# A sum's limit on another engine, quotients behind a small reciprocal, and weights scaled by another engine, in a two-layer convolution kernel

## The chip, the cores and the metric

The kernel runs on one core of one Trainium2 chip. The metric is the device time of one execution in microseconds (us); the time of a version is the median of its runs. The core has TensorE (PE, matrix products), VectorE (DVE), ScalarE (ACT), GpSimd (POOL) and queues for transfers. Each engine works through its own instructions in the order in which they stand in its program, and waits at an instruction until what it needs is there.

## The reference, cut to what matters

The input is 8 images of 256 channels of 64x64 pixels. Two layers are added to it in turn, each on a group-normalised input. Layer 0 makes 9 weights per pixel and channel group from small convolutions and applies them to a 3x3 neighbourhood. Layer 1 has an attention over a 7x7 neighbourhood and a dynamic convolution, whose part is what the change touches:

```python
# layer 0: 1x1 convolutions of the normalised input
x1 = _conv1x1(x, w1, b1)
x2 = _conv1x1(x, w2, b2)
x3 = _conv1x1(x, w3, b3)
...
# layer 1
wts = jnp.einsum('oc,bchw->bohw', Wfc, x).reshape(b, C, kc2, h, w)
wts = jax.nn.softmax(wts, axis=2)
...
oc = _dwconv(hid, w2).reshape(b, kc2, C, h, w)
out_conv = jnp.sum(oc * wts.transpose(0, 2, 1, 3, 4), axis=1)
return rate1 * out_att + rate2 * out_conv
```

The nine copies of `oc` that the softmax weighs are equal, so the kernel makes one. It takes the exponentials of eight differences to the ninth logit, adds them and 1 into `tot`, limits that, and weighs `oc` with `tot` times its reciprocal `rec`. In layer 0 the normalisation is folded into the weights: `w12` and `w3` are multiplied per input channel by `sc`, once for each image.

## The kernel before, in words

An image is cut into 8 bands of 8 rows (512 pixels). Channels lie on the 128 partitions in two tiles, `ct` 0 and 1. The main loop goes over bands `g` and in each over 8 steps `s`; `ct = s // 4` and `m = s % 4`. I call the four steps of one `ct` a half. In one iteration, layer 1 of band `g` is worked on, and layer 0 of a band twelve ahead, so that both layers share the engines.

The order of the work is written out by hand. A step has six places, one for each call of `advance()`; a function handed to `after(n, f)` is put into the programs n places later. So a number in `after` is a position in every engine's queue and not a time.

In each step:

- TensorE applies the attention weights of two steps before (`sco`, L747), makes this step's scores (`sco`, L703), transposes the probabilities of the step before (`ptp`, L735), and makes two products with the weights of the dynamic convolution (`pf`, L825, each shown as four matmuls of 128x512); then come layer 0's products (`p` L369, `pw` L447, `ph` L429) and the maps of queries, keys and values (`pq` L637, `pk` L658, `pv` L563).
- VectorE takes the scores' maximum (`prob`, `nmax`, L712), adds attention values to the output (`xr`, L757), does taps of two depthwise convolutions (`acc`, L782 and L808), and inverts the sum of the attention's exponentials. This is the small reciprocal: `tot`, L727, two columns. It also makes the products of layer 0 (`prod`, L460).
- ScalarE copies the transposed probabilities (`pt`, L737), makes the attention's exponentials (`prob`, L720), the exponentials of `pf` (`ex`, L830, twice a step), and multiplies the probabilities by the small reciprocal (`prob`, L729). In its order these stand as L737, L720, first L830, L729.
- GpSimd adds layer 0's products up (`xg`, L468) and the exponentials of a half's steps (`ex`, L1026).

At the end of a half (m = 3) `dynamic_sum` follows, which the change touches. Its parts before, by the step counted from the half's last one, which is step 0:

- step 1, place 2: GpSimd adds the two columns of `ex` (L838) into `tot`, which is `ex[:, 1]`.
- step 2, place 1: `quotient`: VectorE adds 1 and limits the sum (L845), and inverts the first half of it (L846). At place 4 `second` inverts the other half (L850). I call this step A.
- place 0 that ends step 2: `weigh`: GpSimd multiplies (L855, L856) and adds to the output (L857). The step that follows is B, and the one after it C.

The tile `ex` has three buffers and each step takes one: the `ex` of step B is written by L830 into the buffer that L855 and L856 of the half have read. `rec` has one buffer, `prod` two, and the PSUM tiles tagged `gen` five.

For `ct` 0 step A is `s` 5 of the same band, for `ct` 1 it is `s` 1 of the next band. Step `s` 0 of a band also starts the small maps of layer 0 (`p`, L328), whose eight evictions (L343, L347) ScalarE does in step 0 and 1.

`scaled_weights` is called once an image; its `scale` multiplies `w12` and `w3` (L296, L297), two tiles each.

Of the kernel before, what the change touches and what calls it, by code (L numbers as in the profile page):

```python
# [12 lines left out]
AF = mybir.ActivationFunctionType  # L13
ALU = mybir.AluOpType
# [72 lines left out]
def conv_layers_kernel(ctx: ExitStack, tc: tile.TileContext, ins: dict, out: bass.AP):  # L87
    nc = tc.nc
# [18 lines left out]
    def load(name, shape, src=None, now=True):  # L107
        t = const.tile(shape, F32, name=f"c_{name}")
        late.append(lambda: nc.scalar.dma_start(out=t, in_=ins[name] if src is None else src))
        if now:  # L110
            late.pop()()
        return t
# [5 lines left out]
    w12 = load("w12", [P, NCT, 2 * REL], ins["w12"].rearrange("(t p) n -> p t n", p=P))  # L118
    w3 = load("w3", [P, NCT, C], ins["w3"].rearrange("(t p) n -> p t n", p=P))
# [95 lines left out]
    def after(n, f):  # L215
        later.append((place[0] + n, f))
# [8 lines left out]
    def gn_affine(sts, means, name, done):  # L225


        n = len(sts)
        mv = stat.tile([P, n, 2], F32, name=f"mv_{name}", tag=f"mv{n}")
        for ct, st in enumerate(sts):  # L230
            nc.vector.bn_aggr(mv[:, ct, :], st)
        mean, var = mv[:, :, 0], mv[:, :, 1]
        gm, d, sc, bi = (stat.tile([P, n], F32, name=f"{v}_{name}", tag=f"{v}{n}") for v in ("gm", "d", "sc", "bi"))

        def group_means(v, k):
            pg = ps.tile([P, n], F32, name=f"pg_{name}_{k}", tag="gen", bufs=5)
            nc.tensor.matmul(pg, means, v, start=True, stop=True)
            return pg


        def a1():
            pg = group_means(mean, 0)
            after(2, lambda: a2(pg))

        def a2(pg):
            nc.vector.tensor_copy(gm, pg)
            for ct in range(n):
                c = slice(ct, ct + 1)
                nc.vector.tensor_scalar(d[:, c], pg[:, c], mean[:, c], None, ALU.subtract)
                nc.vector.tensor_scalar(d[:, c], d[:, c], d[:, c], var[:, c], ALU.mult, ALU.add)  # L250
            after(5, a3)

        def a3():
            pg = group_means(d, 1)
            after(2, lambda: a4(pg))

        def a4(pg):
            nc.vector.tensor_scalar(sc, pg, GN_EPS, None, ALU.add)
            after(2, a5)

        def a5():
            nc.scalar.activation(sc, sc, AF.Sqrt)
            after(4, a6)

        def a6():
            nc.vector.reciprocal(sc, sc)
            for ct in range(n):
                c = slice(ct, ct + 1)
                nc.vector.tensor_scalar(bi[:, c], gm[:, c], sc[:, c], -1.0, ALU.mult, ALU.mult)
            done(sc, bi)  # L270

        after(3, a1)
# [15 lines left out]
    def scaled_weights(b):  # L288

        im = images[b]  # L290

        def scale(sc, bi):
            im.w12s = w0.tile([P, NCT, 2 * REL], F32, tag="w12s", name=f"w12s_{b}", bufs=1)
            im.w3s = w0.tile([P, NCT, C], F32, tag="w3s", name=f"w3s_{b}", bufs=1)
            for kt in range(NCT):
                nc.vector.tensor_scalar(im.w12s[:, kt], w12[:, kt], sc[:, kt : kt + 1], None, ALU.mult)  # L296
                nc.vector.tensor_scalar(im.w3s[:, kt], w3[:, kt], sc[:, kt : kt + 1], None, ALU.mult)  # L297
            after(5, lambda: through(bi))

        def through(bi):  # L300
            pb = ps.tile([P, 1 + NCT], F32, tag="gen", name=f"pb_{b}", bufs=5)
            for m, to, w in ((0, 0, w12), (0, 64, w12), (1, 0, w3[:, :, :P]), (2, 0, w3[:, :, P:])):
                for kt in range(NCT):
                    nc.tensor.matmul(
                        pb[to : to + w.shape[2], m : m + 1], w[:, kt], bi[:, kt : kt + 1],
                        start=(kt == 0), stop=(kt == NCT - 1),
                    )
            after(2, lambda: biases(pb))

        def biases(pb):  # L310
            im.bias = w0.tile([P, 1 + NCT], F32, tag="bias", name=f"bias_{b}")
            nc.vector.tensor_add(im.bias[:, 0:1], pb[:, 0:1], par[:, PB21 : PB21 + 1])
            for ct in range(NCT):
                nc.vector.tensor_add(
                    im.bias[:, 1 + ct : 2 + ct], pb[:, 1 + ct : 2 + ct], chan[:, ct, CB3 : CB3 + 1]
                )

        gn_affine([im.st0[:, ct] for ct in range(NCT)], gmat, f"a{b}", scale)

    def small_maps(b, i):  # L320
# [396 lines left out]
    def exponentials(nm, prob, nmax):  # L717
        tot = w1.tile([P, 2], F32, tag="tot", name=f"tot_{nm}", bufs=4)
        for h in range(2):
            nc.scalar.activation(  # L720
                prob[:, h, :NKEY], prob[:, h, :NKEY], AF.Exp, bias=nmax[:, h : h + 1], scale=-1.0,
                accum_out=tot[:, h : h + 1],
            )
        return tot
# [107 lines left out]
    def dynamic_sum(b, i, ct, ex, oc):  # L832

        tot = ex[:, 1]
        xr = images[b].xr[i]

        engine = nc.vector if (b, i, ct) == (B - 1, NB - 1, NCT - 1) else nc.gpsimd
        engine.tensor_add(tot, tot, ex[:, 0])  # L838
        rec = w1.tile([P, BAND], F32, tag="rec", name=f"rec_{b}_{i}_{ct}", bufs=1)
        n = BAND // 2  # L840

        def quotient():


            nc.vector.tensor_scalar(tot, tot, 1.0, 1.0e37, ALU.add, ALU.min)  # L845
            nc.vector.reciprocal(rec[:, :n], tot[:, :n])  # L846
            after(3, second)

        def second():
            nc.vector.reciprocal(rec[:, n:], tot[:, n:])  # L850
            after(2, weigh)

        def weigh():

            engine.tensor_mul(tot, tot, rec)  # L855
            engine.tensor_mul(oc, oc, tot)  # L856
            engine.tensor_add(xr[:, ct], xr[:, ct], oc)  # L857
            if ct == NCT - 1:
                after(6, store)

        def store():
            nc.sync.dma_start(
                out=out[b].rearrange("(t p) n -> p t n", p=P)[:, :, i * BAND : (i + 1) * BAND], in_=xr
            )

        after(5, quotient)


    def beside(g, s):
# [93 lines left out]
    with tc.manual_schedule():  # L963
# [21 lines left out]
        for g in range(-AHEAD, B * NB):  # L985
            b, i = divmod(g, NB)
            for s in range(STEPS):
# [3 lines left out]
                if g >= 0:  # L991
# [9 lines left out]
                    tot = exponentials(nm, prob, nmax)  # L1001
# [21 lines left out]
                if g >= 0:  # L1023
                    branch_weights(b, i, ct, m, 1, ex)
                    if exb is not None:
                        after(4, lambda ex=ex, exb=exb: nc.gpsimd.tensor_add(ex, ex, exb))  # L1026
                    if m == 1:
                        conv[1]()
                        conv = depthwise_middle(b, i, ct)
                    if m == NT // 2 - 1:  # L1030
                        oc = depthwise_end(b, i, ct, conv[1])
                        after(4, lambda a=(b, i, ct, ex, oc): dynamic_sum(*a))
# [97 lines left out]
```

## Time and profile before

| What | Value |
|---|---|
| Median of 3 runs | 4154.88 us (4153.21 to 4155.15) |
| Span of the profiled run, granted TensorE clock | 4150.9 us, 0.993 |
| Busy in all: PE, DVE, ACT, POOL | 4022.6, 3591.9, 3081.0, 2923.0 us |
| Busy from 1000 to 2000 us: PE, DVE, ACT, POOL | 988.9, 896.7, 773.0, 749.2 us |
| L845, limit of the sum, DVE, 128x512 | 128 times, mean 1070 ns, median 418 ns |
| L846 and L850, reciprocals, DVE, 128x256 | 128 times each, means 1753 and 1746 ns |
| L727, small reciprocal, DVE, 128x2 | 512 instructions, mean 159 ns |
| L296 and L297, scaling, DVE, 128x64 and 128x256 | 16 times each, means 997 and 1060 ns |
| L838, L855, L856, L857, GpSimd, 128x512 | 127 times each, 1272 to 1278 ns |
| L468, GpSimd, 128x1024 | 549 times, mean 2193 ns |

In the table a mean far above the median says that some instructions of a kind take much longer than others of the same form. The busy time of PE has ends that are modelled, so waits of PE are better read from the starts of its instructions. In the lines of the waits view, "A <- B" says that A's engine stood idle before A until B released it; the figures are the total, the count and, last, the longest.

### The profile page before, as it was taken

The page shows a single profiled execution, that of the slowest core. Times are in us where ns is not written, and L with a number is a line of the kernel's source. Part 1 is how long each engine was busy: PE and PEld are TensorE (multiplying, and loading weights), DVE is VectorE, ACT ScalarE, POOL GpSimd, SP SyncE. Part 2 cuts the span into 40 slices and gives each one's busy share as a digit, 9 for nine tenths or more (in the row PEclk, how much of TensorE's full clock was granted, in tenths as well). Part 3 has the DMA queues.
Part 4 walks back from the last instruction along what each step waited for, and adds up shares of the span by engine and source line. Part 5 has one row for each costly group of instructions (what it writes and reads, how often), then busy time and mean ns, then how long its engine had stood idle before and what let it go on. Part 6 is the DMA issues. An engine that isn't in the chain of part 4 may idle for free.

```text
span 4150.9 us, 72735 instructions
## 1 busy us (share of the span) xinstructions
PE 4022.6 (97%) x25292; PEld 2126.8 (51%) x25292; DVE 3591.9 (87%) x7248; ACT 3081.0 (74%) x7726; POOL 2923.0 (70%) x1902
## 2 busy tenths in 40 slices
PE   6789999999999999999999999999999999999998
PEld 3345555555555555555555555555555555455554
DVE  5878998899898898889998898888988889977777
ACT  3467778777787777877778777777778777687776
POOL 4767777677786777777777777777777677744554
PEclk8999999999999999999999999999999999999999
DMA  8854234234244233334234234244233233111100
GB/s 226 194 135 111 73 91 109 72 94 109 62 101 107 76 94 98 81 94 109 72 85 118 72 94 105 66 101 106 71 82 99 65 87 85 33 41 39 39 28 21
DMA packets 381264, 367.89 MB, mean 89 GB/s; under 512 B 55648, under 2 KB 282720, under 8 KB 380640
## 3 DMA queue, kind: packets, MB, share of 16 engines
q1 hardware_dynamic: 377568, 358.68, 34.3%
q8 instruction: 200, 3.28, 0.3%
q10 hardware_dynamic: 3328, 4.55, 0.3%
q14 instruction: 168, 1.38, 0.1%
HBM read 261.42 MB, written 101.71 MB: 87 GB/s over the span
## 4 chain that ended last, share of the span: by engine, by line
PE 71%; DVE 14%; POOL 6%; ACT 5%; DMA 2%; issue 2%; SPq 1%; POOLq 0%; ACTq 0%; DVEq 0%
PE pf L825 33%; PE ptp L735 5%; PE sco L747 5%; PE pk L658 5%; PE sco L703 5%; PE p L369 5%; DVE prod L460 4%; PE pq L637 4%; POOL xg L468 3%; PE pvt L607 2%; PE pv L563 2%; DVE acc L808 2%; PE pw L447 2%; DVE acc L782 2%; POOL ex L1026 2%
## 5 line engine op out<-in xcount | busy, mean ns | idle before, releaser
L825 PE MATMUL pf<-yp,c_wfc 128*128 128x512 f32 x4096 | 1930.5, 595 | 10.6 <-ACT vc L581 5.0
L468 POOL TENSOR_TENSOR xg<-xg,prod 128x1024 f32<-128x1024 f32 x549 | 1203.9, 2193 | 96.6 <-DVE prod L460 64.1
L825 PEld LDWEIGHTS pf<-yp,c_wfc 128*128 128x128 f32 x4096 | 729.9, 190 | 690.5 <-issue 619.4
L1026 POOL TENSOR_TENSOR ex<-ex,ex 128x1024 f32<-128x1024 f32 x384 | 907.7, 2364 | 61.9 <-ACT ex L830 57.2
L830 ACT ACTIVATE ex<-pf 128x512 f32<-128x512 f32 x1024 | 607.3, 593 | 297.9 <-POOL ex L1026 141.3
L782 DVE SCALAR_TENSOR_TENSOR acc<-yp,c_chan,acc 128x504 f32<-128x504 f32 (+3 forms) x1104 | 766.2, 694 | 42.3 <-ACT acc L773 21.7
L460 DVE SCALAR_TENSOR_TENSOR prod<-pw,c_par,x3q 128x1040 f32<-128x1040 f32 x576 | 733.9, 1281 | 66.8 <-PE pw L447 21.6
L808 DVE SCALAR_TENSOR_TENSOR acc<-hid,c_chan,acc 128x504 f32<-128x504 f32 (+3 forms) x1024 | 757.8, 740 | 20.2 <-ACT acc L802 2.1
L855 POOL TENSOR_TENSOR ex<-ex,rec 128x512 f32<-128x512 f32 x127 | 162.3, 1278 | 809.5 <-DVE rec L850 767.1
L729 ACT ACTIVATE prob<-prob,tot 128x196 f32<-128x196 f32 x1024 | 411.6, 450 | 387.2 <-DVE tot L727 386.4
L712 DVE CUSTOM_DVE_ANT_0 prob<-sco,c_mask 128x196 f32<-128x196 f32 x1024 | 325.5, 355 | 272.4 <-PE sco L703 272.0
L720 ACT ACTIVATE prob<-prob,nmax 128x196 f32<-128x196 f32 x1024 | 461.4, 454 | 46.9 <-DVE nmax L712 45.3
L747 PEld LDWEIGHTS sco<-pt,vt 112*64 112x64 f32 x8160 | 283.8, 137 | 182.3 <-issue 51.7
L737 ACT COPY pt<-ptp 112x512 f32<-112x512 f32 x511 | 297.0, 581 | 105.0 <-PE ptp L735 103.0
L735 PE MATMUL ptp<-ident,prob 128*112 128x128 f32 x2044 | 341.7, 287 | 31.2 <-ACT prob L729 30.5
L747 PE MATMUL sco<-pt,vt 112*64 112x64 f32 x8160 | 347.0, 227 | 0.0
L735 PEld LDWEIGHTS ptp<-ident,prob 128*112 128x112 f32 x2044 | 203.9, 133 | 201.4 <-issue 77.7
L703 PE MATMUL sco<-kb,qb 64*64 64x196 f32 x4096 | 295.2, 357 | 0.0
L563 PE MATMUL pv<-yp,c_wv 128*128 128x512 f32 (+2 forms) x576 | 247.3, 554 | 0.6
L369 PE MATMUL p<-xc,w3s 128*128 128x512 f32 x512 | 244.4, 601 | 0.0
L658 PE MATMUL pk<-yp,c_wk 128*128 128x512 f32 (+2 forms) x576 | 240.8, 545 | 0.0
L637 PE MATMUL pq<-yp,c_wq 128*128 128x512 f32 x512 | 240.6, 592 | 0.0
(140 smaller groups left out, 5294.0 us busy)
## 6 DMA issues: line engine op xcount, KB each, us to landing
x<-x3n SPq DMA_DIRECT2D x128, 264.0 KB, 2.1
x3q<-x SPq DMA_DIRECT2D x128, 264.0 KB, 7.2
xc<-in_x SPq DMA_DIRECT2D x64, 512.0 KB, 5.0
xg<-in_x SPq DMA_DIRECT2D x256, 128.0 KB, 4.8
x<-xg SPq DMA_DIRECT2D x256, 128.0 KB, 2.4
yp<-x SPq DMA_DIRECT2D x128, 256.0 KB, 3.3
xr<-x SPq DMA_DIRECT2D x64, 512.0 KB, 5.8
out_x<-xr SPq DMA_DIRECT2D x64, 512.0 KB, 3.1
```

What stands on the lines that cost most here:

```text
L369: nc.tensor.matmul(p3, im.w3s[:, kt, mt * P : (mt + 1) * P], im.xc[i][:, kt, :], start=(kt == 0), stop=(kt == NCT - 1),)
L460: nc.vector.scalar_tensor_tensor(prod[:, :, :RUN], pw[:, j, :RUN].unsqueeze(1).to_broadcast([P, SHARE, RUN]), par[:, PCB2 + k : PCB2 + k + 1],
L468: nc.gpsimd.tensor_add(im.xg[i], im.xg[i], rows(prod))
L703: nc.tensor.matmul(sco[half[t], h, :NKEY], qb[half[h], 2 * m + t].rearrange("p r c -> p (r c)"), kb[half[h], :, c0 : c0 + KW], start=True, ...
L720: nc.scalar.activation(prob[:, h, :NKEY], prob[:, h, :NKEY], AF.Exp, bias=nmax[:, h : h + 1], scale=-1.0, accum_out=tot[:, h : h + 1],)
L735: nc.tensor.transpose(ptp[:, h, ch], prob[:, h, ch * CHUNK : (ch + 1) * CHUNK], ident)
L747: nc.tensor.matmul(po[half[h], :, t * TQ : (t + 1) * TQ], im.vt[i + ch, m][:n, t, (2 * ct + h) * HD : (2 * ct + h + 1) * HD], pt[:n, h, ch ...
L782: nc.vector.scalar_tensor_tensor(o, yp[:, ct, ra + dr : rb + dr, ca + dc : cb + dc], chan[:, ct, CW1 + k : CW1 + k + 1], o, ALU.mult, ALU.add,
L808: nc.vector.scalar_tensor_tensor(o, hid[:, ra + dr : rb + dr, ca + dc : cb + dc], chan[:, ct, CW2 + k : CW2 + k + 1], o, ALU.mult, ALU.add,)
L825: nc.tensor.matmul(pf, wfc[:, kt, 2 * m + j, ct * P : (ct + 1) * P], images[b].yp[i][:, kt, PAD : PAD + R], start=(kt == 0), stop=(kt == N ...
L830: nc.scalar.activation(ex[:, j].rearrange("p (r c) -> p r c", r=R), pf, AF.Exp)
L1026: after(4, lambda ex=ex, exb=exb: nc.gpsimd.tensor_add(ex, ex, exb))
```

## The change

The limit of the sum goes from VectorE to GpSimd and stands right behind the sum it limits (L841 of the changed kernel). The quotient is put in two places later, so that the small reciprocal of that step stands ahead of it on VectorE, and the second half follows it two places later instead of three. The scaling of the 1x1 weights goes from VectorE to ScalarE.

```diff
-                nc.vector.tensor_scalar(im.w12s[:, kt], w12[:, kt], sc[:, kt : kt + 1], None, ALU.mult)
-                nc.vector.tensor_scalar(im.w3s[:, kt], w3[:, kt], sc[:, kt : kt + 1], None, ALU.mult)
+                nc.scalar.activation(im.w12s[:, kt], w12[:, kt], AF.Copy, scale=sc[:, kt : kt + 1])
+                nc.scalar.activation(im.w3s[:, kt], w3[:, kt], AF.Copy, scale=sc[:, kt : kt + 1])
...
         engine.tensor_add(tot, tot, ex[:, 0])
+        engine.tensor_scalar(tot, tot, 1.0, 1.0e37, ALU.add, ALU.min)
...
         def quotient():
-            nc.vector.tensor_scalar(tot, tot, 1.0, 1.0e37, ALU.add, ALU.min)
             nc.vector.reciprocal(rec[:, :n], tot[:, :n])
-            after(3, second)
+            after(2, second)
...
-        after(5, quotient)
+        after(7, quotient)
```

## The prediction, made before the changed kernel was run

> **What bounds the kernel now.** I read the page first: who is busy, and through whom the chain runs.
>
> ```profile
> PE 4022.6 (97%) x25292; PEld 2126.8 (51%) x25292; DVE 3591.9 (87%) x7248; ACT 3081.0 (74%) x7726; POOL 2923.0 (70%) x1902
> ...
> PE 71%; DVE 14%; POOL 6%; ACT 5%; DMA 2%; issue 2%; SPq 1%; POOLq 0%; ACTq 0%; DVEq 0%
> ```
>
> TensorE sets the time, but 29% of the chain is others: somewhere PE waits. Work freed on VectorE is worth only the waits of PE that it ends. I measured these in the PE timeline between 400 and 3900 us, as the start of each group of matmuls less the shortest usual distance from the group before: 88 us in all, about 12.5 us in each image of eight bands (499 us). Of these 64 us lie at the transposes L735 or the pf after them, which need the probabilities of the step before. So I asked who waits in that chain.
>
> ```profile
> POOL ex L855 <- DVE rec L850: 767.1, 119, 15.4
> ...
> ACT prob L729 <- DVE tot L727: 386.4, 266, 6.4
> ...
> ACT ex L830 <- POOL oc L856: 24.5, 58, 1.5
> ```
>
> ScalarE stands before L729 because the small reciprocal L727 comes late; GpSimd stands 767 us idle at L855; and L830, which in ScalarE's order comes ahead of the next L729, already meets GpSimd's L856 with no room left in 58 places. The last line matters most below. Then the timelines. A half of ct 1, first VectorE (start, duration):
>
> ```profile
> 2008.82 0.41 DVE L845 TENSOR_SCALAR ex<-ex 128x512 f32<-128x512 f32 x1
> 2009.27 1.75 DVE L846 RECIPROCAL rec<-ex 128x256 f32<-128x256 f32 x1
> ...
> 2012.30 0.16 DVE L727 RECIPROCAL tot<-tot 128x2 f32<-128x2 f32 x1
> ...
> 2013.87 1.75 DVE L850 RECIPROCAL rec<-ex 128x256 f32<-128x256 f32 x1
> 2015.53 1.20 DVE L460 SCALAR_TENSOR_TENSOR prod<-pw,c_par,x3q 128x1040 f32<-128x1040 f32 x1
> ```
>
> ScalarE in the same half:
>
> ```profile
> 2011.84 0.20 ACT L720 ACTIVATION_READ_ACCUMULATOR prob<-prob,nmax 128x1 f32 x1
> ...
> 2019.08 0.58 ACT L830 ACTIVATE ex<-pf 128x512 f32<-128x512 f32 x1
> 2020.31 0.81 ACT L729 ACTIVATE prob<-prob,tot 128x196 f32<-128x196 f32 x2 [0.65 <-DVE tot L727]
> ```
>
> GpSimd and TensorE there:
>
> ```profile
> 2015.70 1.28 POOL L855 TENSOR_TENSOR ex<-ex,rec 128x512 f32<-128x512 f32 x1 [6.11 <-DVE rec L850]
> 2017.06 1.28 POOL L856 TENSOR_TENSOR oc<-oc,ex 128x512 f32<-128x512 f32 x1
> ```
>
> ```profile
> 2022.66 0.65 PE L735 MATMUL ptp<-ident,prob 128*112 128x128 f32 x4
> ```
>
> L720 ends at 2012.04, so L727 could not have run before that: here the quotient fills a time in which VectorE would have stood. L729 ends at 2021.12 and PE takes its result at 2022.66: 1.5 us to spare.
>
> [...] L845 takes 0.41 us in ct 1 and, in most halves of ct 0, 2.38 us beside an L468 of 2.19 us (mean 1070 ns, median 418). [...]
>
> **The change, part by part.** I set the two programs' instruction orders side by side.
>
> *Scaling.* VectorE loses 15.9 + 17.0 = 32.9 us (L296, L297). [...] It helps VectorE in one half an image.
>
> *The limit.* VectorE loses 136.9 us (L845) and the 33 us wait for L838. GpSimd gains 127 L841. Not in the trace; from below, a copy of 128x420 (L633) takes 536 ns, so 0.65 us for 512 columns; from above a tensor_tensor of 128x512, 1.27. I take 0.8[...]. GpSimd idles there for 5 to 6 us, so its cost is only that L846 of ct 0 may wait for it.
>
> *The quotients.* On VectorE, step A was L845, L846, two taps, L727, two taps, L850, prod, L712; it becomes two taps, L727, L846, two taps, L850, prod, L712. On GpSimd weigh slips one place: in 107 of 127 halves an L468 now stands ahead of L855, and it needs the prod that comes after L850.
>
> ct 1, the half shown: the taps end at 2010.3, L727 waits for L720 until 2012.1, and L846 is queued behind it. L846 12.2 to 13.9, taps to 15.35, L850 to 17.05 (15.62 before). Prod +1.2 = 18.2; L468 +2.2 = 20.4; L855 and L856 +2.63 = 23.1 (18.34 before). L830 of step B waits for that: 23.1 instead of 19.08. Behind it in ScalarE's queue L729 starts 0.5 later, ends 24.4 instead of 21.12. PE can begin its transposes about 0.28 before that end, at 24.1: it stands 1.5 us. The next pf needs the bank that L641, behind L729, frees: 0.4 more, as the ct 0 half at 2053 shows now. The same sum over the rows of the other halves of ct 1 gives 1.3 to 1.8 us in 41 of 54 (the rest have 3.4 us to spare, or no L343 queue): 62 us, with the 0.4 each 78 us. The last ten bands' halves mostly have no L468; there nothing moves the end.
>
> ct 0, the half around 2039: L845 went (2.38 us), L727 comes at 2040.6 instead of 2044.9. PE's waits for that L729 end: 1.5, 0.6 and 1.5 us in each of seven images, 25 us. The later wait, at step C, is 0.41 + 0.44 us in 36 halves. There L838 ended at 2039.44; GpSimd runs 0.6 later against PE after ct 1 (its unbroken run starts 2.55 later, PE stands 1.9), L841 0.8, so L846 at 2040.85 (2041.88 before). Two taps and L727 (1.48) now stand ahead of it, so L850 ends 1.03 + 1.48 = 2.5 earlier, 2045.7. Prod 46.9, L468 49.1, L856 51.75 (50.94): L830 0.8 later, but L729, which waited for L727 until 2052.92, at 52.25. That frees about 0.65 of the 0.85: 36 x 0.65 = 23 us.
>
> Sum: +78 - 25 - 23 = +30 us: 4154.9 + 30 = 4185.
>
> **Rivals.** *Faster.* The GpSimd delay is absorbed and only gains count: -25 - 36 x 0.85 = -56, 4099. For it: VectorE loses 170 us of work and waits, and L729's wait for L727 is 386 us, which the new order attacks directly. Against: L830 stands ahead of L729 in one queue, and its buffer waits for L856. If half the loss comes, 39 - 48 = -9: 4146.
>
> *No change.* Losses and gains cancel within 8 us, 4147 to 4163; nothing couples them, so it is a matter of sizes.
>
> *Worse.* L841 at 1.27 us and GpSimd's lag keep step C's waits of ct 0 and lengthen them by 0.5: 78 - 25 + 18 = +71, 4226. For it: GpSimd has hardly a gap from 2015.70 to 2039.44 in the trace.
>
> *VectorE becomes the bound* by its idle time at L727, 1.7 us in 41 halves: no, it waits for PE's scores 272 us in all, before L712, and catches up there.
>
> **How the numbers follow.** The forecast 0.51; worse 0.20; faster 0.20; no change 0.09. Slower is the first two: 0.71. From the half-absorbed and full gains down to 4125 and up past the worse case to 4235 I leave out some 0.1 below and 0.05 above, and what the hand sums miss in how a wait of PE moves the next.
>
> **What would show it.** Right: in the waits, L830 on L856 rises from 24.5 to over 150 us; L727 on L720 rises from 10.1 to about 70; the wait for L845 is gone; L729 on L727 falls to below half of 386; L855's on L850 falls, taken over by L468 waiting for prod; on GpSimd L468 stands between L841 and L855; PE's idle time at L735 on L729 (107.6 us with its weight loads) rises, in the third step of a band. A step is wrong if L841 takes over 1.3 us, or if L846 of ct 1 doesn't wait behind L727. The forecast is wrong if L830 waits for L856 below 50 us: then ScalarE is not held, and the time falls under 4147.

## The result, and the profile after

| Version | Median, us | Ratio to before, 95% interval |
|---|---|---|
| before | 4155.01 (4153.21 to 4155.57, 4 runs) | |
| changed | 4278.88 (4275.14 to 4283.07, 4 runs) | 1.0299 [1.0281, 1.0317] |

The changed kernel is 124 us slower: the direction is as forecast, but the loss is four times the 30 us that I worked out, and outside the range. First the page of the changed kernel: busy time by engine, the shares of the chain that ended last, and the group of the new instruction (busy us and mean ns after the bar).

```profile
PE 4063.0 (95%) x25292; PEld 2139.7 (50%) x25292; DVE 3419.2 (80%) x7089; ACT 3089.4 (72%) x7758; POOL 3147.0 (74%) x2029
...
PE 28%; POOL 22%; DVE 18%; ACT 17%; issue 11%; DMA 2%; SPq 1%; POOLq 0%; DVEq 0%; ACTq 0%
...
L841 POOL TENSOR_SCALAR ex<-ex 128x512 f32<-128x512 f32 x127 | 243.6, 1918 | 11.1
```

VectorE lost 173 us of work, as intended. TensorE's share of the chain fell from 71% to 28%: in this profile the end hangs on GpSimd, VectorE and ScalarE as well. That share alone doesn't show the loss, for two variants below that are faster than the kernel before have 34% and 41%. L841 takes 1918 ns, where the forecast has 0.8 us and 1.27 as its upper bound. The waits of the changed kernel (total us, times, longest):

```profile
POOL xg L468 <- DVE prod L460: 651.0, 134, 10.7
...
ACT ex L830 <- POOL oc L856: 365.1, 122, 3.6
...
DVE tot L727 <- ACT prob L720: 208.2, 162, 2.1
...
PEld ptp L735 <- ACT prob L729: 151.1, 186, 2.7
...
POOL ex L855 <- DVE rec L850: 119.6, 16, 8.0
...
PE ptp L735 <- ACT prob L729: 101.4, 84, 2.3
...
DVE rec L846 <- POOL ex L841: 85.6, 42, 3.2
...
ACT prob L729 <- DVE tot L727: 51.2, 78, 1.1
...
PE pvt L607 <- ACT ex L830: 14.4, 6, 2.4
```

The kernel before has no line for the last of these; four of the others stand there as

```profile
PEld ptp L735 <- ACT prob L729: 77.1, 171, 3.0
...
POOL xg L468 <- DVE prod L460: 64.1, 32, 10.9
...
PE ptp L735 <- ACT prob L729: 30.5, 56, 2.7
...
DVE tot L727 <- ACT prob L720: 10.1, 18, 1.8
```

L830, which waited 24.5 us in 58 places for L856, now waits 365.1 us in 122, nearly every half. L855's wait for L850 has become L468's wait for `prod`. The gain is that L729 waited 386.4 us for L727 and now 51.2. VectorE stands 85.6 us for the limit, where it stood 32.9 us for the sum (L845 for L838). The last line is a new place at which TensorE stands, once in each of six images, until L830 releases it. The timelines of two neighbouring halves show how these join, first VectorE (start, duration, operation, the idle time before it and its releaser). The lines up to 2085 belong to `ct` 1, the last to `ct` 0:

```profile
2080.22 0.17 DVE L727 RECIPROCAL tot<-tot 128x2 f32<-128x2 f32 x1 [1.73 <-ACT prob L720]
2080.31 1.73 DVE L846 RECIPROCAL rec<-ex 128x256 f32<-128x256 f32 x1
...
2083.32 1.75 DVE L850 RECIPROCAL rec<-ex 128x256 f32<-128x256 f32 x1
2084.98 1.20 DVE L460 SCALAR_TENSOR_TENSOR prod<-pw,c_par,x3q 128x1040 f32<-128x1040 f32 x1
...
2111.88 1.75 DVE L846 RECIPROCAL rec<-ex 128x256 f32<-128x256 f32 x1 [1.82 <-POOL ex L841]
```

GpSimd over the same stretch, `ct` 1 first, then `ct` 0 from 2108 on:

```profile
2086.27 2.19 POOL L468 TENSOR_TENSOR xg<-xg,prod 128x1024 f32<-128x1024 f32 x1 [8.65 <-DVE prod L460]
2088.41 1.27 POOL L855 TENSOR_TENSOR ex<-ex,rec 128x512 f32<-128x512 f32 x1
2089.76 1.27 POOL L856 TENSOR_TENSOR oc<-oc,ex 128x512 f32<-128x512 f32 x1
...
2108.57 1.27 POOL L838 TENSOR_TENSOR ex<-ex 128x512 f32<-128x512 f32 x1
2109.93 1.92 POOL L841 TENSOR_SCALAR ex<-ex 128x512 f32<-128x512 f32 x1
...
2117.86 2.19 POOL L468 TENSOR_TENSOR xg<-xg,prod 128x1024 f32<-128x1024 f32 x1 [2.04 <-DVE prod L460]
...
2121.36 1.27 POOL L856 TENSOR_TENSOR oc<-oc,ex 128x512 f32<-128x512 f32 x1
```

And what this does to ScalarE, then to TensorE:

```profile
2091.07 0.60 ACT L830 ACTIVATE ex<-pf 128x512 f32<-128x512 f32 x1 [3.18 <-POOL oc L856]
2091.56 0.80 ACT L729 ACTIVATE prob<-prob,tot 128x196 f32<-128x196 f32 x2
...
2122.66 0.60 ACT L830 ACTIVATE ex<-pf 128x512 f32<-128x512 f32 x1 [3.58 <-POOL oc L856]
2123.15 0.80 ACT L729 ACTIVATE prob<-prob,tot 128x196 f32<-128x196 f32 x2
```

```profile
2092.07 0.78 PE L735 MATMUL ptp<-ident,prob 128*112 128x128 f32 x4 [1.16 <-ACT prob L729]
...
2123.66 0.78 PE L735 MATMUL ptp<-ident,prob 128*112 128x128 f32 x4 [1.26 <-ACT prob L729]
```

In both halves the chain is the same: L850 late, `prod` behind it, GpSimd standing at L468 with L855 and L856 queued behind, L830 waiting for its buffer, L729 queued behind L830, TensorE standing at its transposes. In `ct` 1 that was forecast. In `ct` 0 it was not: there L846 starts only when L841 ends, at 2111.85, and this lateness goes through the same chain to 2123.66.

The clock is a second loss. In windows of the changed kernel from 1149 to 1165 us (stretch, length, busy us of PE, PEld, DVE, ACT, POOL with counts, granted TensorE clock, DMA share, GB/s):

```profile
1149.00:1152.00 3.00, 1.67 (x29) 1.06 (x27) 2.96 (x5) 0.99 (x3) 2.84 (x3) 1.00 0.03 5
1152.00:1154.00 2.00, 1.85 (x6) 0.93 (x7) 1.97 (x8) 2.00 (x5) 2.00 (x2) 0.75 0.00 0
1154.00:1156.00 2.00, 2.00 (x4) 0.89 (x3) 0.75 (x2) 1.21 (x5) 2.00 (x2) 0.50 0.00 0
1156.00:1158.00 2.00, 2.00 (x5) 0.76 (x4) 0.00 (x0) 1.18 (x3) 2.00 (x3) 0.89 0.00 0
1158.00:1165.00 7.00, 7.00 (x53) 3.98 (x52) 5.07 (x14) 4.30 (x12) 6.84 (x4) 1.00 0.33 76
```

After the wait that ends at 1152.01 the granted clock falls to half (0.50 from 1154 to 1156) and comes back some 3.4 us later. TensorE's timeline there shows what it costs:

```profile
1152.01 0.78 PE L735 MATMUL ptp<-ident,prob 128*112 128x128 f32 x4 [1.34 <-ACT prob L729]
1152.93 3.68 PE L825 MATMUL pf<-yp,c_wfc 128*128 128x512 f32 x4
...
1158.17 1.88 PE L825 MATMUL pf<-yp,c_wfc 128*128 128x512 f32 x4
```

Four matmuls take 3.68 us instead of 1.88. Between 400 and 3700 us the changed kernel has 19 such drops, the kernel before has one. By their length in the trace, 3.41 us at half the clock, each costs about 3.4 / 2 = 1.7 us of TensorE's work, together 19 x 1.7 = 32 us, an estimate.

### The profile page after: what moved, and what is told of

Read it like the earlier page. It is cut to its first block, busy times and chain, and to the rows that moved or that the text cites. A ratio compares the mean times of both kernels' runs of the same rounds, so it can differ in the third digit from the quotient of the medians.

```text
span 4280.2 us, 72696 instructions
## 1 busy us (share of the span) xinstructions
PE 4063.0 (95%) x25292; PEld 2139.7 (50%) x25292; DVE 3419.2 (80%) x7089; ACT 3089.4 (72%) x7758; POOL 3147.0 (74%) x2029
## 4 chain that ended last, share of the span: by engine, by line
PE 28%; POOL 22%; DVE 18%; ACT 17%; issue 11%; DMA 2%; SPq 1%; POOLq 0%; DVEq 0%; ACTq 0%
PE pf L825 13%; POOL xg L468 8%; DVE prod L460 5%; DVE acc L782 4%; DVE rec L846 4%; POOL ex L1026 3%; POOL oc L856 3%; POOL ex L855 3%; PE pk L658 3%; ACT prob L729 3%; ACT ex L830 3%; ACT x L343 2%; ACT prob L720 2%; PE sco L747 2%; POOL ex L841 2%
## 5 line engine op out<-in xcount | busy, mean ns | idle before, releaser
L825 PE MATMUL pf<-yp,c_wfc 128*128 128x512 f32 x4096 | 1962.7, 603 | 12.4 <-ACT ex L830 3.9
L468 POOL TENSOR_TENSOR xg<-xg,prod 128x1024 f32<-128x1024 f32 x549 | 1201.7, 2189 | 676.9 <-DVE prod L460 651.0
L830 ACT ACTIVATE ex<-pf 128x512 f32<-128x512 f32 x1024 | 608.4, 594 | 641.1 <-POOL oc L856 365.1
L720 ACT ACTIVATE prob<-prob,nmax 128x196 f32<-128x196 f32 x1024 | 463.0, 458 | 60.6 <-DVE nmax L712 59.6
L729 ACT ACTIVATE prob<-prob,tot 128x196 f32<-128x196 f32 x1024 | 409.5, 450 | 51.2 <-DVE tot L727 51.2
L735 PE MATMUL ptp<-ident,prob 128*112 128x128 f32 x2044 | 343.8, 288 | 101.4 <-ACT prob L729 101.4
L735 PEld LDWEIGHTS ptp<-ident,prob 128*112 128x112 f32 x2044 | 204.0, 134 | 274.0 <-ACT prob L729 151.1
L846 DVE RECIPROCAL rec<-ex 128x256 f32<-128x256 f32 x128 | 222.7, 1740 | 85.6 <-POOL ex L841 85.6
L855 POOL TENSOR_TENSOR ex<-ex,rec 128x512 f32<-128x512 f32 x127 | 161.5, 1272 | 155.1 <-DVE rec L850 119.6
L841 POOL TENSOR_SCALAR ex<-ex 128x512 f32<-128x512 f32 x127 | 243.6, 1918 | 11.1
L727 DVE RECIPROCAL tot<-tot 128x2 f32<-128x2 f32 x512 | 82.3, 161 | 209.1 <-ACT prob L720 208.2
```

Source lines behind the costliest of these rows:

```text
L468: nc.gpsimd.tensor_add(im.xg[i], im.xg[i], rows(prod))
L720: nc.scalar.activation(prob[:, h, :NKEY], prob[:, h, :NKEY], AF.Exp, bias=nmax[:, h : h + 1], scale=-1.0, accum_out=tot[:, h : h + 1],)
L729: nc.scalar.activation(prob[:, h, :NKEY], prob[:, h, :NKEY], AF.Copy, scale=tot[:, h : h + 1])
L735: nc.tensor.transpose(ptp[:, h, ch], prob[:, h, ch * CHUNK : (ch + 1) * CHUNK], ident)
L825: nc.tensor.matmul(pf, wfc[:, kt, 2 * m + j, ct * P : (ct + 1) * P], images[b].yp[i][:, kt, PAD : PAD + R], start=(kt == 0), stop=(kt == N ...
L830: nc.scalar.activation(ex[:, j].rearrange("p (r c) -> p r c", r=R), pf, AF.Exp)
```

## The experiments

The forecast's theory, A in the expectations: the place of `weigh` behind an L468 makes L856 late, and this reaches TensorE through L830 and L729. Its rivals: B, the work and lateness that L841 adds on GpSimd; C, the reciprocals queued behind L727. Each diff is against the changed kernel unless it says otherwise.

**The limit back on VectorE, all else kept.**

```diff
-        engine.tensor_scalar(tot, tot, 1.0, 1.0e37, ALU.add, ALU.min)
...
         def quotient():
+            nc.vector.tensor_scalar(tot, tot, 1.0, 1.0e37, ALU.add, ALU.min)
```

> The changed kernel with the limit back on VectorE, inside quotient, behind L727. Theory A (an L468 ahead of L855 on GpSimd makes L856 late, so L830 and behind it L729 on ScalarE are late and PE stands): the queue order is unchanged, so it stays slow, 4250 to 4310 us, L830 waiting for L856 above 300 us; the limit behind L727 costs ct 1 its 0.4 us[...]. Theory B (GpSimd's new work, 127 x 1.92 us of L841, is the cost): back near 4150 us. Theory C (the reciprocals that now wait for L727, VectorE idle 208 us there, are the cost): as slow as the changed kernel, about 4290 us.

Measured: 4334.55 us, ratio 1.0426 [1.0411, 1.0442], with L830 waiting 369.8 us for L856. This is far from theory B's 4150 us, and above the range that I gave theory A. So the move of the limit by itself isn't the cause. With the limit on VectorE (L845, mean 863 ns) in the delayed quotient the loss is 56 us larger: the clock drops 36 times, 17 more than in the changed kernel, about 29 us (granted clock 0.977 in the profiled run, against 0.984), and TensorE waits 124.9 us at the transposes instead of 101.4. Theory C, with about 4290 us, is not excluded by this run.

**The limit alone, on the kernel before.**

```diff
         engine.tensor_add(tot, tot, ex[:, 0])
+        engine.tensor_scalar(tot, tot, 1.0, 1.0e37, ALU.add, ALU.min)
...
-            nc.vector.tensor_scalar(tot, tot, 1.0, 1.0e37, ALU.add, ALU.min)
             nc.vector.reciprocal(rec[:, :n], tot[:, :n])
```

> The kernel before with one edit, the limit on GpSimd right behind L838; quotients and weights as before. Theory A: weigh keeps its place ahead of L468, GpSimd is idle there anyway, VectorE gains its 0.4 to 2.4 us a half: 4130 to 4156 us, L830's wait for L856 stays below 60 us. Theory B: most of the loss, 4230 us or more. Theory C: no loss, about 4155 us or less.

Measured: 4131.04 us, 0.9935 [0.9921, 0.9950]. With the quotient in its old place the limit on GpSimd is a gain of 24 us, at the same 1920 ns for one, and although L846 waits 130.0 us for it in 63 places. L830's wait for L856 stays at 27.6 us. Theory C expects no loss here either, so this run speaks against B alone.

**`weigh` one place earlier**, so that L855 and L856 stand ahead of that L468 again:

```diff
             nc.vector.reciprocal(rec[:, n:], tot[:, n:])
-            after(2, weigh)
+            after(1, weigh)
```

> The changed kernel with weigh one place after second instead of two, so that L855 to L857 stand ahead of L468 again; the limit stays on GpSimd and the quotient behind L727. Theory A: L856 of ct 1 ends some 3.4 us earlier, within PE's slack, and ct 0 too; the gains at step A and C are left: 4095 to 4130 us, below the kernel before; L830's wait for L856 well under 200 us, PE's idle time at L735 under 60 us (252 in the changed kernel, weight loads included), and the granted clock in the steady part without drops. Theory B: GpSimd's work is the same, 4250 us or more. Theory C: L846 still waits for L727, VectorE idle there 200 us, 4250 us or more.

Measured: 4107.96 us (4106.34 to 4112.04), 0.9885 [0.9868, 0.9901]. One place in the order is worth 171 us, more than the whole loss. Its waits:

```profile
POOL ex L855 <- DVE rec L850: 560.4, 116, 8.0
...
ACT prob L729 <- DVE tot L727: 185.3, 179, 1.8
...
DVE rec L846 <- POOL ex L841: 98.2, 51, 3.6
...
ACT ex L830 <- POOL oc L856: 34.4, 70, 1.6
...
PE ptp L735 <- ACT prob L729: 1.8, 3, 1.2
```

GpSimd still stands idle for VectorE, 560.4 us, and L846 waits for L841 longer than in the changed kernel (98.2 us against 85.6); neither brings the loss back. L830's wait is back to 34.4 us and TensorE's at the transposes to 1.8. The granted clock, 0.994 over the span, doesn't drop once between 400 and 3700 us. This is theory A: B and C both expected 4250 us or more.

**`weigh` earlier in one `ct` only**, to see which half loses: in `ct` 1 with `after(2 - ct, weigh)`, in `ct` 0 with `after(1 + ct, weigh)`.

```diff
-            after(2, weigh)
+            after(2 - ct, weigh)
```

> The changed kernel with weigh one place earlier in halves of ct 1 alone. Theory A: ct 1's waits of PE go, about 1.25 us in 41 halves = 50, while those of ct 0 stay, 1.4 + 0.44 us in some 36 halves: 4215 to 4235 us, with drops of the granted clock still there. If ct 0 were not part of the loss, as the forecast had it: about 4125 us.

```diff
-            after(2, weigh)
+            after(1 + ct, weigh)
```

> The changed kernel with weigh one place earlier in halves of ct 0 alone. Theory A: ct 0's waits go with the drops of the clock, ct 1's stay: 4108 + 41 x 1.25 = 4160 us, 4145 to 4175, L830 waiting for L856 about half of the changed kernel's 365 us, no drops of the clock. If the forecast's shares were right and ct 1 made the loss: near 4250 us.

Measured: early in `ct` 1 gives 4238.11 us, 1.0199 [1.0184, 1.0215]; early in `ct` 0 gives 4170.64, 1.0037 [1.0023, 1.0050]. L830's wait for L856 is cut in about half in each (211.0 and 189.5 us), but the first gains 41 us and the second 108. The late `weigh` costs most in `ct` 0, where the forecast had a gain. The two gains add up to 149 us and not to 171, and the first time is 3 us above the range that I gave: with `weigh` early in `ct` 1, TensorE's waits in `ct` 0 grow to about 1.8 us each (70.9 us in 43 places at L735 in the waits view). With `ct` 0 mended no clock drop is left (granted clock 0.994); with `ct` 1 mended there are 28 (0.982).

**A cheaper instruction in the limit's place.** It leaves out the 1 and the limit:

```diff
-        engine.tensor_scalar(tot, tot, 1.0, 1.0e37, ALU.add, ALU.min)
+        engine.tensor_copy(tot, tot)
```

> The changed kernel with a GpSimd copy of 128x512 in place of the limit (the 1 and the limit are left out), expected at 0.65 us against 1.92. Theory A: ct 1 stands as before, about 1.2 us in 41 halves; ct 0's L846 comes 1.3 us earlier and its wait at step C falls from 1.4 us to some 0.2: 4185 to 4215 us, so that the forecast was off mainly by the price of L841. Theory B: the loss falls in proportion to the work, two thirds of it: about 4195 us, so this run alone does not tell A from B. Theory C: unchanged, about 4275 us.

Measured: 4187.89 us (4185.69 to 4188.92), 1.0073 [1.0058, 1.0088]. The instruction's group and the waits:

```profile
L841 POOL COPY ex<-ex 128x512 f32<-128x512 f32 x127 | 77.4, 610 | 8.1
```

```profile
ACT ex L830 <- POOL oc L856: 364.9, 122, 3.6
...
PE ptp L735 <- ACT prob L729: 53.1, 56, 1.2
...
DVE rec L846 <- POOL ex L841: 29.5, 42, 1.9
```

1.3 us less at L841 is worth 91 us, about as much as the forecast fell short by (94 us). The first line warns against reading a wait's total as its cost: L830 waits the same 365 us, 122 times. What differs is whether its end reaches TensorE: that wait falls from 101.4 to 53.1 us, and no clock drop is left (granted clock 0.994). The waits in `ct` 1 are as long as in the changed kernel (1.23 us from start to start over the usual distance); those at the transposes in `ct` 0 are gone or at 0.6.

**The same with the addition but no limit**, a size between the two:

```diff
-        engine.tensor_scalar(tot, tot, 1.0, 1.0e37, ALU.add, ALU.min)
+        engine.tensor_scalar(tot, tot, 1.0, None, ALU.add)
```

> The changed kernel with L841 cut to one operation, the add of 1 (the limit is left out). It measures what GpSimd asks for one and for two operations. If one operation takes half, near 1 us, theory A puts the time between e5 and the changed kernel, at about 4215 us; if the cost is that of any tensor_scalar, 1.9 us and 4279 us.

Measured: L841 1490 ns, 4241.70 us, 1.0208 [1.0194, 1.0222], 6 clock drops (granted clock 0.989). Both sizes that I expected were off, but the time lies between the two kernels, as theory A has it. Time rises with the price of the one instruction: 610, 1490 and 1918 ns give 4188, 4242 and 4279 us. The traces show where. In the first three rows, TensorE's waits at the transposes and at the `pf` behind them are taken from start to start over the usual distance, between 250 and 3700 us; the fourth is from the waits view; the last is half the time of the clock drops between 400 and 3700 us.

| TensorE loses, us | before | copy, 610 ns | add only, 1490 ns | changed, 1918 ns |
|---|---|---|---|---|
| `ct` 0, behind L729 of step A | 33.5 | 0 | 0 | 0 |
| `ct` 0, step C | 28.5 | 28.0 | 62.6 | 76.5 |
| `ct` 1, step C | 0 | 57.1 | 57.9 | 55.9 |
| at L607, for L830 | 0 | 6.4 | 11.8 | 14.4 |
| drops of the clock | 1.7 | 0 | 10.2 | 32.4 |
| sum | 63.7 | 91.5 | 142.5 | 179.2 |

The rows of `ct` 0's step C, of L607 and of the clock follow the price of L841; that of `ct` 1 doesn't. From column to column the sum grows by 28, 51 and 37 us, and the time by 33, 54 and 37.

**Scaling alone**, on the kernel before:

```diff
-                nc.vector.tensor_scalar(im.w12s[:, kt], w12[:, kt], sc[:, kt : kt + 1], None, ALU.mult)
-                nc.vector.tensor_scalar(im.w3s[:, kt], w3[:, kt], sc[:, kt : kt + 1], None, ALU.mult)
+                nc.scalar.activation(im.w12s[:, kt], w12[:, kt], AF.Copy, scale=sc[:, kt : kt + 1])
+                nc.scalar.activation(im.w3s[:, kt], w3[:, kt], AF.Copy, scale=sc[:, kt : kt + 1])
```

> The kernel before with one edit, the weights scaled by ScalarE. VectorE loses 33 us of L296 and L297, ScalarE gains about 7 (4 instructions of 0.34 and 0.50 us an image, overlapping). Theory A: worth at most the waits of PE in the one half of an image in which L845 stood behind them, 0 to 8 us: 4147 to 4157 us. A rival that holds the scaling responsible for part of the loss: above 4165 us.

Measured: 4147.23 us (21 runs), 0.9982 [0.9975, 0.9988]: a small gain of 8 us. The instructions take 338 and 495 ns on ScalarE.

**The limit on VectorE and `weigh` earlier**, which fills the square of the limit's place and `weigh`'s place (both edits above):

```diff
-        engine.tensor_scalar(tot, tot, 1.0, 1.0e37, ALU.add, ALU.min)
...
+            nc.vector.tensor_scalar(tot, tot, 1.0, 1.0e37, ALU.add, ALU.min)
...
-            after(2, weigh)
+            after(1, weigh)
```

> e1 with weigh one place earlier: the limit on VectorE, behind L727. With e1, e4 and the changed kernel it makes two by two of the limit's place and of weigh's place. Theory A: the place of weigh is worth about 170 us either way, and the limit on VectorE[...] costs some 20 to 40 us more than on GpSimd: 4125 to 4150 us. If the limit's place were the main thing: above 4250 us.

Measured: 4156.07 us, 1.0001 [0.9993, 1.0010]. The place of `weigh` is worth what I expected; the limit on VectorE (L845, mean 1114 ns) costs 48 us over GpSimd here, more than the 20 to 40 that I gave it.

| us | `weigh` two places behind | one place behind | difference |
|---|---|---|---|
| limit on VectorE | 4334.55 | 4156.07 | 178 |
| limit on GpSimd | 4278.88 | 4107.96 | 171 |
| difference | 56 | 48 | |

The two effects nearly add up, and `weigh`'s place is three times the other. The cell in the first row with `weigh` one place behind has the quotient behind L727 and the scaling on ScalarE, and is as fast as the kernel before: with the limit on VectorE, moving the quotient gains nothing. It hardly loses anything either, so theory C is not needed for the loss. With the limit on GpSimd the same two moves, of the quotient and of the scaling, take 4131.04 us to 4107.96; the scaling may have 8 of that.

**The limit in two halves of 256 columns**, with `weigh` earlier, so that L846 waits only for the half that it reads:

```diff
-        engine.tensor_scalar(tot, tot, 1.0, 1.0e37, ALU.add, ALU.min)
+        for h in (slice(0, BAND // 2), slice(BAND // 2, BAND)):
+            engine.tensor_scalar(tot[:, h], tot[:, h], 1.0, 1.0e37, ALU.add, ALU.min)
...
-            after(2, weigh)
+            after(1, weigh)
```

> e4 (weigh one place earlier) with the limit in two instructions of 256 columns, so that L846 can start after the first. A candidate for the best version. L846 of ct 0 waits 98 us for L841 in 51 places in e4; half of an L841, some 0.9 us, comes off each[...]. If what is left of PE's waits hangs on it: 4090 to 4102 us; if they are already within PE's slack: 4104 to 4112 us.

Measured: 4085.52 us (4082.73 to 4090.34), 0.9830 [0.9815, 0.9845], the fastest version that keeps the limit, and below both ranges that I expected. The reciprocal's first half (L847 in this kernel) waits 58.2 us for the limit instead of 98.2, though GpSimd works 27 us longer:

```profile
L842 POOL TENSOR_SCALAR ex<-ex 128x256 f32<-128x256 f32 x254 | 270.5, 1065 | 21.2
```

**A copy in the limit's place with `weigh` earlier** (the 1 and the limit left out), a bound for what the limit still costs there:

```diff
-        engine.tensor_scalar(tot, tot, 1.0, 1.0e37, ALU.add, ALU.min)
+        engine.tensor_copy(tot, tot)
...
-            after(2, weigh)
+            after(1, weigh)
```

> e4 with a GpSimd copy (0.61 us) for the limit (the 1 and the limit are left out): what the price of L841 is worth once weigh stands ahead of L468. Theory A: PE's waits are mostly gone there already, so little, 4085 to 4105 us, against the 91 us that the same edit was worth in the changed kernel (4279 to 4188).

Measured: 4086.28 us, 0.9833 [0.9817, 0.9850]. The limit in halves is as good as a copy. The same 1.3 us at L841 are worth 22 us here and 91 in the changed kernel: with `weigh` ahead of that L468, most of L841 is hidden.

Not run: a fourth buffer of `ex`, with which L830 would not have to wait for L856. It would test this link by itself; here it is shown by the waits that come and go with the place of `weigh`.

## Why the prediction was right in direction and wrong in size

*What bounds the kernel, and who holds it.* Right: L830 on L856, named as the line that matters most, is where the loss passes. Undoing the one place of `weigh` takes away the wait and the loss.

*Scaling.* Costed at nothing but for one VectorE half an image; alone it gains 8 us.

*The quotients, `ct` 1.* The mechanism was right, the term too large. L727 waits for L720 and L846 runs behind it (2080.22, 2080.31 above), L468 stands ahead of L855, TensorE stands. I had 1.5 + 0.4 us; measured are 1.23 and, for the second, about 0.1. In 41 halves that is about 54 us (55.9 in the table above), not 78. The sign that L727 would wait for L720 "about 70" us fits the step A of `ct` 1, where it waits 84.6. Most of the rest of the 208.2, 94.3 us, lies in the steps C, where L720 itself is late; with `weigh` one place earlier 0.9 us of that is left. So that part follows from the loss and is not its cause.

*The limit, and with it the quotients of `ct` 0: the step that failed.* The term "L841 0.8" was mis-sized. The 0.8 us was my estimate, between the 0.65 us that the copy L633 of 128x420 (536 ns) gives for 512 columns and a tensor_tensor of the same tile, 1.27 us, which I thought its upper bound; no trace had shown it. L841 measured 1.92 us; what I had priced was in effect a copy (0.61 us measured), not a tensor_scalar. The prediction named 1.3 us as the sign of a wrong step. In `ct` 0 L846 has no room: the 1.12 us that L841 takes longer pass to L846, L850, `prod`, L468, L856, L830 and L729. The gain at step C of "36 x 0.65 = 23 us" became a loss: TensorE's 0.41 + 0.44 us there are now mostly 1.40 + 0.44, and it stands at the transposes there in 43 halves instead of 35. The table has 28.5 us before and 76.5 after: 48 us lost, a swing of 71. To this come the 14.4 us at L607. The gain at step A did come, 33.5 us where I had 25, with L729's wait for L727 down to 51.2 us.

The copy and the add show that this term is the cause, and not only beside it: they change L841 alone, and the time follows it. That the copy's 4187.89 us lies 3 from the forecast is in part luck. I had taken 0.8 us and not 0.61; a straight line between the copy and the add gives some 4200 us for 0.8, an estimate. So the price explains about 79 of the 94 us. And two misses of the sum cancel in the copy: `ct` 1 loses 57 us instead of 78, and the gain of 23 at step C is not there (28.5 to 28.0).

*What the forecast didn't have: the granted clock.* 19 drops, 32 us. The copy has none, so they hang on L841's price too. From the copy to the changed kernel, 91 us, TensorE's waits at the transposes and the `pf` behind them add 47, those at L607 8, and the drops 32; about 3 are not placed. From the forecast, 94 us: +71 for step C, +14 for L607, +31 for the clock, -22 for `ct` 1 and -8 for step A, which leaves about 8 that are not placed.

*The rivals.* "Worse" named the right place, step C of `ct` 0, with L841 at 1.27 us. For that price the line between the copy and the add gives some 4228 us, an estimate, so its 4226 fits; it was too low because the price was higher still. "Faster", 4099 us, is close to what the old place of `weigh` gives, 4107.96. "VectorE becomes the bound" did not happen: its busy share fell to 80%.

## What to carry to other kernels

When an edit moves the reader of a shared buffer one place behind other work in an in-order queue, follow the buffer to its next writer and to what is queued behind that writer: here one place was worth 171 us, and the kernel was slower although every engine that the edit meant to relieve was relieved. Price a moved instruction from a measured one of the same operation on the same engine; if there is none, give the range a far end above the nearest other operation, and see what the chain does at that end. Where the consumer works in halves, produce in halves: here that took 4107.96 us to 4085.52.

## What the runs showed of the hardware that was not expected

- On GpSimd, for 128x512 f32, a tensor_scalar with two operations takes 1918 ns, with one 1490, a copy 610, while the tensor_tensor L838 takes 1271. So the tensor_scalar with its one input isn't cheaper than that tensor_tensor with two. For 128x256 the two operations take 1065 ns.
- In the trace of the changed kernel TensorE, which is 95% busy, has its granted clock drop to half 19 times between 400 and 3700 us, for 3.41 us at a time, after waits of 1.28 to 2.40 us. The drops start whole multiples of 3.413 us apart (those at 828.75, 958.46, 1088.16 and 1153.02 us are 38, 38 and 19 of these lengths apart). I laid stretches of 3.413 us on that grid, so that each drop fills one. In the 19 stretches just ahead of a drop TensorE stood 1.43 to 2.02 us by the trace; of the 928 other stretches at full clock only 3 have as much, up to 1.76. What makes the clock drop the traces don't show; that it goes with the idle time of a stretch is how these figures read.
- So a wait's place seems to count, and not only its length. The wait of 1.34 us that ends at 1152.01 lies in a stretch with 1.48 us idle, and the clock drops at the stretch's end. The wait of 1.26 us that ends at 2123.66 lies in one with 1.40, and it doesn't (granted clock 1.00 up to 2135). A wait of 1.87 us that ends at 1348.89 is divided by a stretch's start, which leaves 1.46, and no drop follows. The figures don't part the two cases sharply, since the ends of TensorE's work are modelled: the 3 stretches with as much and no drop have 1.46, 1.75 and 1.76 us.
